# Layer 0's experts in two groups of batch elements

## The chip, the core and the metric

The kernel runs on one core of a Trainium2 chip. A core has a matrix engine (PE; its weight loads are shown apart as PEld), a vector engine (DVE), a scalar engine (ACT), a general one (POOL), and a queue engine (SP) that issues most transfers. Each engine works through its own instructions in order and waits for others on semaphores. Transfers run on 16 DMA engines that the queues share. The time is the device time of the whole program in microseconds (us), from the runs without a profile; the profile is one further execution, recorded instruction by instruction.

## What is computed

`x` has 16 batch elements of 128 tokens and 128 features. Four layers follow each other, each with an attention-like part and a feed-forward part, each added to `x` with a gate. The change touches layer 0. Its first part is a mixture of experts: a context picks two of eight experts for each token; its second part is a feed-forward whose hidden values are rounded to 8 bits.

```
logits = ctx @ Wg + bg                       # 8 experts
scores, idx = top_k(logits, 2); weights = softmax(scores)
h = relu(norm(x) @ W1[e] + b1[e])            # for the chosen experts e
x = x + tanh(g_xattn[0]) * sum(weights * (h @ W2[e] + b2[e]))

h = quantize(relu(norm(x) @ w1.T + b1))      # feed-forward of layer 0
x = x + tanh(g_ffn[0]) * quantize(h @ quantize(w2).T + quantize(b2))
```

Layer 1 follows with a block-sparse attention over `norm(x)` and the context.

## The kernel before

**Routing** (`l0_xattn`, lines 302 to 451). The normed rows of `x` are written to memory (`rows_d`). The two best experts of each token are found for all 16 batch elements at once. The 4096 pairs of token and expert are sorted by expert into blocks of 128 rows; each expert begins at a new block, so at most 2x16 + 7 = 39 blocks (`NBLK`) are needed. A running count over batch elements (`upto`, with `on` as its restart mask) gives each expert's number of blocks (`blocks`) and its last block (`ends`), `base` and `place` the row of each pair, `row` and `rows` the place from which its result is fetched later. `of` (the block of each pair, one-hot) and `os` (the row in it, one-hot) are multiplied on PE to turn this around: `tok` lists which row of `x` stands in which place of which block. The expert of each block is loaded into registers on SP, ACT and DVE (`numbers`).

**Blocks** (lines 453 to 504). `pipeline` runs four stages over the 39 blocks. At step t it calls `fetched(t)`, `turned(t-4)`, `hidden(t-5)` and `output(t-6)`. `fetched` gathers 128 rows by an indirect DMA from POOL (`l0_xs`, 4 buffers) and loads the expert's first weights, 258 KB, into one of `DEPTH = 7` places of `l0_w1` (tag `w16a`). `turned` transposes the rows and copies the second weights out of `w2` (tag `w16b`). `hidden` and `output` are two products of four 128x128 steps each, every one two passes on PE; `output` adds the bias and writes 64 KB to `out_d`. Every third block also lets one *position gather* go (`k.gather`): 65 gathers that fill `pe` for layer 2 and are spread over layers 0 and 1, each behind a given instruction.

**Returns** (`l0_returned`). For each batch element two indirect DMAs from POOL fetch the rows of both experts from `out_d`, and DVE adds each, weighted, to `x`. By `behind`, a gather waits for the add of the gather two before it. A return reads `out_d` as a whole and so waits for all blocks.

**Feed-forward** (`l0_ffn`). It goes by chunks of four batch elements. `hidden(j)` norms a chunk (with a square root on ACT), multiplies by `w1` (four 128x512 products of two passes), and rounds to 8 bits on ACT; `output(j)` multiplies by `w2` and adds to `x`. The returns of the next chunk are issued between the products. `turn_positions` transposes four matrices of `pe` and scales them, with PE and ACT; six such turns stand in chunks 1 to 3, eleven in layer 1's feed-forward.

**PSUM.** Eight banks are dealt out by tags, `mm=4, tr=2, acc=2`; a tag's banks go round. Before layer 1, `k.banks(bank=8)` closes this pool and opens one with a single tag.

**Order.** The program is written in the order of the calls; the build (`schedule_with_timeline_sim=True`) then places instructions in each engine's queue by a simulated time line, so that something written later can stand earlier if it is ready. The order is fixed when the kernel runs.

Of the kernel before, what the change touches and what calls it, by code (L numbers as in the profile page):

```python
# [63 lines left out]
class Kernel:  # L64


    def __init__(self, ctx, tc, a):
        self.tc, self.nc, self.a = tc, tc.nc, a
        pool = lambda name, bufs, **kw: ctx.enter_context(tc.tile_pool(name=name, bufs=bufs, **kw))
        self.const = pool("const", 1)  # L70
        self.wts = pool("weights", 1)
        self.work = pool("work", 2)
        self.small = pool("small", 3)
        self.psum_stack = ctx.enter_context(ExitStack())
        self.banks(mm=4, tr=2, acc=2)
# [206 lines left out]
def pipeline(n, *stages):  # L282
# [3 lines left out]
    for t in range(n + max(lag for _, lag in stages)):  # L286
        for s, (fn, lag) in enumerate(stages):
            u = t - lag
            if 0 <= u < n:
                kept[u, s] = fn(u, kept.pop((u, s - 1))) if s else fn(u)  # L290

def l0_xattn(k):

    nc = k.nc
    NBLK = 2 * NB + NE - 1  # L300
    M = 1.5 * 2.0**23
# [13 lines left out]
    nc.vector.memset(on, 1.0)  # L315
    nc.vector.memset(on[:, :, 0:1], 0.0)

# [43 lines left out]

    blocks, ends = k.sm([P, NE], "l0_blocks", bufs=1), k.sm([P, NE], "l0_ends", bufs=1)
    nc.vector.tensor_scalar(blocks, upto[:, :, NB - 1], 1.0 / P, 63.5 / P, ALU.mult, ALU.add)
# [36 lines left out]
    for n in range(2 * NB):  # L400
# [15 lines left out]
    ended = k.w2k("l0_ended")[:, : NBLK * NE].rearrange("p (n e) -> p n e", e=NE)  # L416
    nc.vector.tensor_tensor(
        ended, bc(k.iota[:, 0:NBLK].unsqueeze(2), [P, NBLK, NE]), bc(ends.unsqueeze(1), [P, NBLK, NE]), ALU.is_ge
    )
    whose = k.sm([P, NBLK], "l0_whose", bufs=1)  # L420
# [3 lines left out]
    k.l0_rows = rows = k.sm([P, 2 * NB], "l0_rows", I32, bufs=1)  # L424
    nc.vector.tensor_copy(rows, row)

# [16 lines left out]
    for n in range(0, NBLK, STEP):  # L443
        _, v = nc.values_load_multi_w_load_instructions(
            expert[0:1, n : n + STEP], [mybir.EngineType.SP, mybir.EngineType.Activation, mybir.EngineType.DVE],
            min_val=0, max_val=NE - 1,
            skip_runtime_bounds_check_because=known,
        )
        numbers += v
    out_d = k.dram.tile([NBLK * P, P], F32, name="l0_out_d")  # L450
    k.l0_out_d = out_d

# [37 lines left out]
    def output(n, args):  # L490
# [8 lines left out]
        )  # L499
        nc.sync.dma_start(out=out_d[n * P : (n + 1) * P], in_=y)  # L500
        if n % 3 == 2:
            k.gather(done)

    pipeline(NBLK, (fetched, 0), (turned, 4), (hidden, 5), (output, 6))


def l0_returned(k, b):
# [3 lines left out]
    for i in range(2):  # L511
        y = k.small.tile([P, P], F32, tag="l0_xs", name="l0_back", bufs=4)
        dma = nc.gpsimd.indirect_dma_start(  # L513
            out=y, out_offset=None, in_=k.l0_out_d,
            in_offset=bass.IndirectOffsetOnAxis(ap=k.l0_rows[:, 2 * b + i : 2 * b + i + 1].bitcast(U32), axis=0),
# [28 lines left out]

def l0_ffn(k):

# [42 lines left out]

    pipeline(NJ, (hidden, 0), (output, 1))  # L590

def l1_xattn(k):
# [8 lines left out]
    nc = k.nc  # L603
    k.banks(bank=8)
    H, DH, G = 16, 8, 4
# [187 lines left out]
def l1_ffn(k):  # L793
# [105 lines left out]
    for s in range(C * NJ + 24):  # L899
# [19 lines left out]
        for m, i in ms:  # L919
# [9 lines left out]
            elif i == C + 3:  # L929
                for fn, half in (  # L930
# [51 lines left out]
def l2_xattn(k):  # L982
# [239 lines left out]

    pipeline(NB // 2, (decays, 0), (scores, 1), (values, 2), (normed, 2), (added, 3))
    k.positions_stack.close()
# [3 lines left out]
def l2_ffn(k):  # L1228
# [85 lines left out]

    pipeline(NB, (one_hot, 0), (gather, 1))

# [24 lines left out]

    pipeline(2 * NE, (hidden, 0), (output, 1))

# [396 lines left out]

LAYERS = [l0_xattn, l0_ffn, l1_xattn, l1_ffn, l2_xattn, l2_ffn, l3_xattn]

# [85 lines left out]
```

## Time and profile before

| | us |
|---|---|
| runs without a profile: median of 3 (lowest, highest) | 897.01 (896.29, 897.06) |
| the profiled execution, whole | 889.87 |
| its span, first to last instruction | 888.2 |
| busy in the span: PE, PEld | 723.8, 483.2 |
| busy: DVE, ACT, POOL | 511.0, 402.5, 434.9 |
| mean granted clock of PE | 0.913 |
| first gather of a block, first product of a block | 47.1, 50.4 |
| last block written to `out_d`, first return issued | 132.0, 135.7 |
| last add of a return (start), last add of layer 0's feed-forward (start) | 191.7, 205.4 |
| first transpose of layer 1, first POOL operation of layer 1 | 203.7, 208.3 |

The three costliest POOL groups that matter here: 65 position gathers at 993 ns, 39 block gathers at 953 ns, 32 returns at 973 ns; that is the time POOL spends on issuing, not the transfer. A row of the time line has the start, the busy time, the engine, the line, the operation, the output and input names (numbers left out, so `l_xs` is `l0_xs`), and in brackets the idle time before it with what ended it. "Granted clock" is the share of full speed that PE was given. A stage's row in the table by windows has each engine's busy time and its count of instructions.

### The profile page before, as it was taken

The numbers are of one execution on the slowest core, as the hardware profiler recorded it, in microseconds if no ns is written. First come the engines' busy times: TensorE is split into PE (matmuls) and PEld (weight loads), VectorE is DVE, ScalarE is ACT, GpSimd is POOL, SyncE is SP. The second block draws the span as 40 slices with busy tenths as digits, with TensorE's granted clock in tenths as the row PEclk, the third lists the DMA queues.
The fourth block names the chain that finished last, engine by engine and source line by source line (L and its number), as shares of the span: only waits on it lengthen the run. The fifth ranks groups of instructions, "written<-read, shape, count | busy, mean of one in ns | idle before, by whom it ended". The sixth has DMA issues, their size and how long they took to land.

```text
span 888.2 us, 13281 instructions
## 1 busy us (share of the span) xinstructions
PE 723.8 (81%) x4349; PEld 483.2 (54%) x4349; DVE 511.0 (58%) x1450; ACT 402.5 (45%) x1006; POOL 434.9 (49%) x455
## 2 busy tenths in 40 slices
PE   3279990667897999899679799994789987999997
PEld 3179990343454555443268733333578885555555
DVE  5735543564645556788967235556541276777863
ACT  0035530332533545777316905631554455666552
POOL 6666655523754774777856603434120043555430
PEclk9989995876998999899959889996799999999999
DMA  8758861100000000000202203332000000000001
GB/s 256 208 131 212 206 157 39 41 22 16 16 16 20 22 25 22 0 0 1 71 25 85 73 3 97 94 83 94 0 1 1 1 1 1 1 1 0 1 1 48
DMA packets 43653, 46.49 MB, mean 52 GB/s; under 512 B 8368, under 2 KB 32560, under 8 KB 43456
## 3 DMA queue, kind: packets, MB, share of 16 engines
q1 hardware_dynamic: 37088, 35.63, 13.7%
q0 software_dynamic: 4384, 8.95, 4.4%
q10 hardware_dynamic: 2112, 1.05, 0.4%
q8 instruction: 35, 0.57, 0.3%
q14 instruction: 34, 0.28, 0.1%
HBM read 40.90 MB, written 4.72 MB: 51 GB/s over the span
## 4 chain that ended last, share of the span: by engine, by line
PE 50%; DVE 20%; POOL 7%; issue 7%; ACT 5%; DMA 4%; SPq 1%; POOLq 0%; DVEq 0%; ACTq 0%
PE ps_bank L38 17%; PE ps_bank L112 16%; PE ps_mm L112 10%; PE ps_acc L112 5%; POOL l_back L513 2%; DMA l_cm<-l_gm_d 2%; DMA l_back<-l_out_d,l_rows 2%; POOL l_ss L1212 2%; ACT l_cm L1155 2%; DVE l_m L38 2%; DVE l1f_r L38 1%; PE ps_bank L116 1%; DVE xnT L38 1%; PE ps_tr L116 1%; DVE l_up L38 1%
## 5 line engine op out<-in xcount | busy, mean ns | idle before, releaser
L962 POOL DMA_INDIRECT pe<-in_L_xattn_rpe,itokT x65 | 64.5, 993 | 63.1 <-DVE l_top L691 20.7
L38 PE MATMUL ps_bank<-xnT,l1f_w 128*128 128x512 f32 x128 | 62.5, 618 | 0.4 <-ACT pe L38 0.4
L691 DVE TENSOR_REDUCE l_top<-ps_bank 128x8 f32<-128x512 f32 x64 | 39.7, 683 | 34.1 <-PE ps_bank L112 34.1
L112 PE MATMUL ps_mm<-pe,ident 128*128 128x512 f32 x64 | 58.9, 1050 | 0.0
L723 ACT ACTIVATE l_a<-ps_bank 128x512 f32<-128x512 f32 x64 | 33.2, 602 | 45.8 <-PE ps_bank L112 45.7
L485 DVE TENSOR_SCALAR l_h<-ps_mm,l_w 128x128 f32<-128x128 f32 x117 | 33.7, 344 | 33.0 <-ACT l_h L487 32.1
L1148 POOL TENSOR_SCALAR_AFFINE_SELECT l_cm<-l_cm 128x512 f32<-128x512 f32 x32 | 23.7, 756 | 58.3 <-DMA l_cm<-l_gm_d 57.0
L1155 ACT ACTIVATE l_cm<-l_cm,l_g 128x128 f32<-128x128 f32 x128 | 39.8, 400 | 25.5 <-POOL l_cm L1148 25.5
L455 POOL DMA_INDIRECT l_xs<-l_rows_d,l_tok x39 | 37.2, 953 | 21.3 <-PE ps_acc L112 14.1
L112 PE MATMUL ps_acc<-l_w,l_h 128*128 128x128 f32 x312 | 45.6, 280 | 1.5 <-DVE l_y L497 1.3
L112 PE MATMUL ps_mm<-l_xT,l_w 128*128 128x128 f32 x312 | 44.4, 280 | 0.4 <-ACT l_xT L470 0.4
L112 PE MATMUL ps_mm<-l_qz,pe 128*128 128x128 f32 x256 | 38.3, 312 | 6.9 <-ACT pe L1102 6.9
L513 POOL DMA_INDIRECT l_back<-l_out_d,l_rows x32 | 31.1, 973 | 25.7 <-DVE x L520 19.0
L112 PEld LDWEIGHTS ps_acc<-l_w,l_h 128*128 128x128 f32 x312 | 40.0, 193 | 2.4 <-ACT l_h L487 2.3
L112 PEld LDWEIGHTS ps_mm<-l_xT,l_w 128*128 128x128 f32 x312 | 40.1, 197 | 0.6 <-ACT l_xT L470 0.6
L112 PEld LDWEIGHTS ps_mm<-l_qz,pe 128*128 128x128 f32 x256 | 36.0, 224 | 8.1 <-ACT pe L1102 8.1
L1328 ACT ACTIVATE l2f_h<-ps_bank,sb_L_ffn_b1T 128x264 f32<-128x264 f32 x64 | 28.1, 482 | 25.8 <-PE ps_bank L112 25.8
L1179 DVE TENSOR_TENSOR l_cm<-ps_mm,l_cm 128x512 f32<-128x512 f32 x32 | 22.0, 687 | 30.7 <-PE ps_mm L112 25.6
L38 PEld LDWEIGHTS ps_bank<-xnT,l1f_w 128*128 128x128 f32 x128 | 24.1, 200 | 24.9 <-issue 17.3
L38 POOL TENSOR_TENSOR l2f_o<-l2f_o,l2f_sc 128x264 f32<-128x264 f32 x9 | 6.5, 727 | 60.0 <-DVE l2f_o L38 57.2
L1337 DVE TENSOR_SCALAR l2f_y<-ps_bank,sb_L_ffn_b2T 128x264 f32<-128x264 f32 x16 | 7.9, 493 | 48.3 <-PE ps_bank L112 48.3
L38 PE MATMUL ps_bank<-xnT,sb_L_xattn_gru_whT 128*128 128x512 f32 x72 | 34.9, 593 | 0.0
(423 smaller groups left out, 1975.2 us busy)
## 6 DMA issues: line engine op xcount, KB each, us to landing
l_w<-in_L_xattn_w1b SPq DMA_DIRECT2D x39, 258.0 KB
l_cm<-l_gm_d SPq DMA_DIRECT2D x64, 128.0 KB
l_out_d<-l_y SPq DMA_DIRECT2D x39, 64.0 KB
sb_L_xattn_W<-in_L_xattn_W SPq DMA_DIRECT2D x1, 2048.0 KB
sb_L_ffn_w<-in_L_ffn_w SPq DMA_DIRECT2D x1, 2048.0 KB
pe<-in_L_xattn_rpe,itokT POOLq DMA_INDIRECT x65, 2.6
x<-in_x ACTq DMA_DIRECT2D x4, 256.0 KB
ctxT<-in_ctxT SPq DMA_DIRECT2D x1, 1024.0 KB
```

What stands on the lines that cost most here:

```text
L38: done = op(*args, **kw)
L112: self.nc.tensor.matmul(out, lhsT, rhs, start=start, stop=stop)
L455: nc.gpsimd.indirect_dma_start(out=xs, out_offset=None, in_=rows_d, in_offset=bass.IndirectOffsetOnAxis(ap=tok[:, n : n + 1].bitcast(U32), ...
L485: nc.vector.tensor_scalar(h[:, cols], ph[:, cols], bias, 0.0, ALU.add, ALU.max)
L513: dma = nc.gpsimd.indirect_dma_start(out=y, out_offset=None, in_=k.l0_out_d, in_offset=bass.IndirectOffsetOnAxis(ap=k.l0_rows[:, 2 * b + i ...
L691: done = nc.vector.tensor_reduce(top[:, 32 * g : 32 * g + 8], ss[g].rearrange("p (n s) -> p n s", n=8), AX.X, ALU.max)
L723: nc.scalar.activation(a, ss[g], AF.Exp, scale=scale)
L962: dma = nc.gpsimd.indirect_dma_start(out=k.pe[:, g if g < G - 1 else P - 1, :], out_offset=None, in_=k.a["L2_xattn_rpe"], in_offset=bass.I ...
L1148: nc.gpsimd.affine_select(out=by_n(cm), in_=by_n(cm), pattern=[[0, 4], [1, P]], compare_op=ALU.is_ge, fill=1e30, base=0, channel_multiplie ...
L1155: nc.scalar.activation(part, part, AF.Exp, scale=-1.0, bias=g[:, n : n + 1])
L1179: nc.vector.tensor_mul(cms[w], ps[w], cms[w])
L1328: nc.scalar.activation(h, ph, AF.Gelu, bias=b1[:, e * NF + f : e * NF + f + 1])
```

## The change

The batch elements are split: the first twelve (`SPLIT`) form group 0, the last four group 1. Each group is sorted into blocks of its own: 2x12 + 7 = 31 and 2x4 + 7 = 15, so `NBLK` is 46. `out_d` becomes two tensors. The restart mask, the block counts, the scans, `base`, `ended` and `rows` are worked out for each group. `of` grows from 39 to 46 columns and moves from a place of its own to the tag `w16a`, which `l0_w1` takes afterwards.

`pipeline` becomes a generator; `l0_xattn` yields for the first time after step 37, when block 31 has been put out, and then after each step. `l0_ffn` receives it and deals out in turn: for each of the first twelve batch elements two returns, one piece of each feed-forward chunk under way (`fed`), one step of the blocks; then the rest of the steps, then the returns of the last four elements, then the last chunk. A chunk is started when its four elements have returned. Its norm now takes the power -0.5 on POOL. Returns have buffers of their own (`l0_back`).

PSUM has one tag of eight banks from the start, and layer 1 opens no pool. Position gathers follow every second block of group 0 (15) in place of every third block (13). Seven position turns stand in layer 0 (one each in chunks 0 to 2, four in chunk 3), ten in layer 1's feed-forward.

```
-        self.banks(mm=4, tr=2, acc=2)
+        self.banks(bank=8)
...
-    NBLK = 2 * NB + NE - 1
+    SPLIT = NB - BJ
+    FIRST = 2 * SPLIT + NE - 1
+    NBLK = 2 * NB + 2 * (NE - 1)
+    groups = ((slice(0, SPLIT), slice(0, FIRST)), (slice(SPLIT, NB), slice(FIRST, NBLK)))
...
-    nc.vector.tensor_tensor_scan(ends, k.ones[:, 0:NE], blocks, 0.0, ALU.mult, ALU.add)
+    for g, (_, ns) in enumerate(groups):
+        nc.vector.tensor_tensor_scan(ends[:, g], k.ones[:, 0:NE], blocks[:, g], float(ns.start), ALU.mult, ALU.add)
...
-    nc.vector.tensor_tensor(base, base, bc(blocks.unsqueeze(2), [P, NE, NB]), ALU.add)
+    for g, (bs, _) in enumerate(groups):
+        part = base[:, :, bs]
+        nc.vector.tensor_tensor(part, part, bc(blocks[:, g].unsqueeze(2), list(part.shape)), ALU.add)
...
-    of = k.work.tile([P, 2 * NB, 2, NBLK], BF16, tag="l0_of", name="l0_of", bufs=1)
+    of = k.wts.tile([P, 2 * NB, 2, NBLK], BF16, tag="w16a", name="l0_of")
...
-        nc.sync.dma_start(out=out_d[n * P : (n + 1) * P], in_=y)
-        if n % 3 == 2:
+        g = int(n >= FIRST)
+        at = n - groups[g][1].start
+        nc.sync.dma_start(out=out_d[g][at * P : (at + 1) * P], in_=y)
+        if n % 2 and not g:
             k.gather(done)
-    pipeline(NBLK, (fetched, 0), (turned, 4), (hidden, 5), (output, 6))
+    for t in pipeline(NBLK, (fetched, 0), (turned, 4), (hidden, 5), (output, 6)):
+        if t >= FIRST + 6:
+            yield
...
-        y = k.small.tile([P, P], F32, tag="l0_xs", name="l0_back", bufs=4)
+        y = k.small.tile([P, P], F32, tag="l0_back", name="l0_back", bufs=4)
...
-    for b in range(BJ):
-        l0_returned(k, b)
     def hidden(j):
-        k.layernorm(j)
...
-            if j + 1 < NJ:
-                l0_returned(k, BJ * (j + 1) + f)
-            if j and f % 2:
-                turn_positions(k, 2 * (j - 1) + f // 2)
+            if j == NJ - 1 or f == 3:
+                turn_positions(k, j if j < NJ - 1 else NJ - 1 + f)
+            if f % 2:
+                yield
...
+    def fed(j):
+        yield from k.norm(j, pow=k.half)
+        yield
+        hq = yield from hidden(j)
+        yield
+        output(j, hq)
+
+    under_way = []
+    for b in range(NB - BJ):
+        l0_returned(k, b)
+        for f in under_way:
+            next(f, None)
+        next(blocks, None)
+        if b % BJ == BJ - 1:
+            under_way.append(fed(b // BJ))
+    for b in range(NB - BJ, NB):
+        next(blocks, None)
+        for f in under_way:
+            next(f, None)
+    for _ in blocks:
+        pass
+    for b in range(NB - BJ, NB):
+        for f in under_way:
+            next(f, None)
+        l0_returned(k, b)
+    for f in under_way + [fed(NJ - 1)]:
+        for _ in f:
+            pass
...
-    k.banks(bank=8)
...
-        if s % 2 and s // 2 <= P // 8 - 6:
-            turn_positions(k, s // 2 + 6)
+        if s % 2 and s // 2 <= P // 8 - 7:
+            turn_positions(k, s // 2 + 7)
...
+def l0(k):
+    blocks = l0_xattn(k)
+    next(blocks)
+    l0_ffn(k, blocks)
```

More of the change, by code (lines that the diff above doesn't have):

```diff
@@ L290, in pipeline @@
                 kept[u, s] = fn(u, kept.pop((u, s - 1))) if s else fn(u)
+        yield t
 def l0_xattn(k):
     nc = k.nc
-    NBLK = 2 * NB + NE - 1
+    SPLIT = NB - BJ
+    FIRST = 2 * SPLIT + NE - 1
+    NBLK = 2 * NB + 2 * (NE - 1)
+    groups = ((slice(0, SPLIT), slice(0, FIRST)), (slice(SPLIT, NB), slice(FIRST, NBLK)))
     M = 1.5 * 2.0**23
@@ L315, in l0_xattn @@
     nc.vector.memset(on, 1.0)
-    nc.vector.memset(on[:, :, 0:1], 0.0)
+    for bs, _ in groups:
+        nc.vector.memset(on[:, :, bs.start : bs.start + 1], 0.0)
     rows_d = k.dram.tile([NB * P, P], F32, name="l0_rows_d")
@@ L360, in l0_xattn @@
     nc.vector.tensor_sub(base, upto, base)
-    blocks, ends = k.sm([P, NE], "l0_blocks", bufs=1), k.sm([P, NE], "l0_ends", bufs=1)
-    nc.vector.tensor_scalar(blocks, upto[:, :, NB - 1], 1.0 / P, 63.5 / P, ALU.mult, ALU.add)
+    blocks, ends = k.sm([P, 2, NE], "l0_blocks", bufs=1), k.sm([P, 2, NE], "l0_ends", bufs=1)
+    for g, (bs, _) in enumerate(groups):
+        nc.vector.tensor_scalar(blocks[:, g], upto[:, :, bs.stop - 1], 1.0 / P, 63.5 / P, ALU.mult, ALU.add)
     nc.vector.tensor_scalar(blocks, blocks, M, None, ALU.add)
     nc.vector.tensor_scalar(blocks, blocks, -M, None, ALU.add)
-    nc.vector.tensor_tensor_scan(ends, k.ones[:, 0:NE], blocks, 0.0, ALU.mult, ALU.add)
+    for g, (_, ns) in enumerate(groups):
+        nc.vector.tensor_tensor_scan(ends[:, g], k.ones[:, 0:NE], blocks[:, g], float(ns.start), ALU.mult, ALU.add)
     nc.vector.tensor_sub(blocks, ends, blocks)
     nc.vector.tensor_scalar(blocks, blocks, float(P), -1.0, ALU.mult, ALU.add)
-    nc.vector.tensor_tensor(base, base, bc(blocks.unsqueeze(2), [P, NE, NB]), ALU.add)
+    for g, (bs, _) in enumerate(groups):
+        part = base[:, :, bs]
+        nc.vector.tensor_tensor(part, part, bc(blocks[:, g].unsqueeze(2), list(part.shape)), ALU.add)
     place = k.sq("l0_place")
@@ L416, in l0_xattn @@
     ended = k.w2k("l0_ended")[:, : NBLK * NE].rearrange("p (n e) -> p n e", e=NE)
-    nc.vector.tensor_tensor(
-        ended, bc(k.iota[:, 0:NBLK].unsqueeze(2), [P, NBLK, NE]), bc(ends.unsqueeze(1), [P, NBLK, NE]), ALU.is_ge
-    )
+    for g, (_, ns) in enumerate(groups):
+        part = ended[:, ns]
+        nc.vector.tensor_tensor(
+            part, bc(k.iota[:, ns].unsqueeze(2), list(part.shape)), bc(ends[:, g].unsqueeze(1), list(part.shape)),
+            ALU.is_ge,
+        )
     whose = k.sm([P, NBLK], "l0_whose", bufs=1)
@@ L424, in l0_xattn @@
     k.l0_rows = rows = k.sm([P, 2 * NB], "l0_rows", I32, bufs=1)
-    nc.vector.tensor_copy(rows, row)
+    for bs, ns in groups:
+        cols = slice(2 * bs.start, 2 * bs.stop)
+        nc.vector.tensor_scalar(rows[:, cols], row[:, cols], -float(P * ns.start), None, ALU.add)
     w = k.sm([P, NB, 2], "l0_w", bufs=1)
@@ L444, in l0_xattn @@
         _, v = nc.values_load_multi_w_load_instructions(
-            expert[0:1, n : n + STEP], [mybir.EngineType.SP, mybir.EngineType.Activation, mybir.EngineType.DVE],
+            expert[0:1, n : min(n + STEP, NBLK)], [mybir.EngineType.SP, mybir.EngineType.Activation, mybir.EngineType.DVE],
             min_val=0, max_val=NE - 1,
@@ L449, in l0_xattn @@
         numbers += v
-    out_d = k.dram.tile([NBLK * P, P], F32, name="l0_out_d")
-    k.l0_out_d = out_d
+    k.l0_out_d = out_d = [
+        k.dram.tile([(ns.stop - ns.start) * P, P], F32, name=f"l0_out{g}_d") for g, (_, ns) in enumerate(groups)
+    ]
     def fetched(n):
@@ L511, in l0_returned @@
     for i in range(2):
-        y = k.small.tile([P, P], F32, tag="l0_xs", name="l0_back", bufs=4)
+        y = k.small.tile([P, P], F32, tag="l0_back", name="l0_back", bufs=4)
         dma = nc.gpsimd.indirect_dma_start(
-            out=y, out_offset=None, in_=k.l0_out_d,
+            out=y, out_offset=None, in_=k.l0_out_d[int(b >= NB - BJ)],
             in_offset=bass.IndirectOffsetOnAxis(ap=k.l0_rows[:, 2 * b + i : 2 * b + i + 1].bitcast(U32), axis=0),
@@ L541, in l2_gates_of_ctx, with l0_ffn @@
     nc.vector.tensor_tensor(k.l2_gc, pg, bc(gb.unsqueeze(1), [P, NB, 2 * H]), ALU.add)
-def l0_ffn(k):
+def l0_ffn(k, blocks):
     nc = k.nc
@@ L588, in output @@
         k.add_chunk(j, y, 4)
-    pipeline(NJ, (hidden, 0), (output, 1))
+    def fed(j):
[25 more added lines that the diff above has]
+            pass
 def l1_xattn(k):
     nc = k.nc
-    k.banks(bank=8)
     H, DH, G = 16, 8, 4
@@ L1221, in added @@
         nc.vector.tensor_tensor(x, x, tb, ALU.add)
-    pipeline(NB // 2, (decays, 0), (scores, 1), (values, 2), (normed, 2), (added, 3))
+    for _ in pipeline(NB // 2, (decays, 0), (scores, 1), (values, 2), (normed, 2), (added, 3)):
+        pass
     k.positions_stack.close()
@@ L1313, in gather @@
         k.copy(tok[:, :, b, :], pg.rearrange("p (e c) -> p e c", e=NE))
-    pipeline(NB, (one_hot, 0), (gather, 1))
+    for _ in pipeline(NB, (one_hot, 0), (gather, 1)):
+        pass
     y = big.tile([P, NB, NE, CAP], F32, name="l2f_y")
@@ L1340, in output @@
         )
-    pipeline(2 * NE, (hidden, 0), (output, 1))
+    for _ in pipeline(2 * NE, (hidden, 0), (output, 1)):
+        pass
     AHEAD = NB * P // W
@@ L1738, in output @@
         k.add_chunk(j, y, 7)
-LAYERS = [l0_xattn, l0_ffn, l1_xattn, l1_ffn, l2_xattn, l2_ffn, l3_xattn]
+def l0(k):
+    blocks = l0_xattn(k)
+    next(blocks)
+    l0_ffn(k, blocks)
+LAYERS = [l0, l1_xattn, l1_ffn, l2_xattn, l2_ffn, l3_xattn]
 @with_exitstack
```

## The prediction

> **What bounds the kernel now.** I read the page's slices of the span first, then the busy time by stage, then the time line of layer 0, then the tiles of the two gathers. In slices of 22 us:
>
> ```profile
> PE   3279990667897999899679799994789987999997
> ...
> POOL 6666655523754774777856603434120043555430
> PEclk9989995876998999899959889996799999999999
> ```
>
> PE is full in slices 3 to 5 (the expert blocks), nearly empty in slice 6 and two thirds busy in 7 and 8, before layer 1 fills it. The stages one by one (columns: busy us of PE, PEld, DVE, ACT, POOL, then clock, DMA share, GB/s):
>
> ```profile
> 62.00:116.00 54.00, 52.50 (x466) 51.99 (x465) 28.65 (x108) 28.35 (x82) 34.66 (x37) 1.00 0.81 211
> ...
> 136.00:192.00 56.00, 25.25 (x100) 13.88 (x100) 26.93 (x101) 13.71 (x22) 30.85 (x32) 0.68 0.15 38
> 192.00:205.00 13.00, 9.03 (x40) 5.58 (x40) 8.09 (x33) 4.78 (x11) 0.00 (x0) 0.76 0.08 21
> ```
>
> The blocks are bound by PE: in the chain of waits three blocks take 5.69 us (98.73 to 104.42), so 1.90 each, at full clock. From 136 to 192 nothing is full. There the chain runs through the 32 returns:
>
> ```profile
> 135.72 3.80 DMA l_back<-l_out_d,l_rows x2
> 139.61 0.36 DVE x L520
> 140.70 0.95 POOL l_back L513
> 141.66 0.72 issue
> 142.60 0.95 POOL l_back L513
> ```
>
> A return waits for the add two returns earlier (`behind`, line 518). One lap, 139.36 to 142.60, is 3.24 us for two returns; the 16 laps from 135.72 to the last add at 192.09 average 3.5. How long a gather takes to land stands under each tile, first the blocks' `l_xs`, then `l_back`:
>
> ```profile
> DMA to landing us min/median/max: 3.1/3.9/5.0
> ```
>
> ```profile
> DMA to landing us min/median/max: 2.4/2.5/2.5
> ```
>
> A gather issued beside the blocks' weight loads lands 1.4 us later than one issued alone. That pair of rows decides most of the forecast. A lap is landing + 0.75: 0.1 to the add, 0.35 for it, 0.3 to the next issue (2.5 + 0.75 = 3.25, the lap seen).
>
> **The head.** It runs from the counts (27.5) to the token list (45.8), all in order on DVE. Added: one more `blocks` op, one more scan, and `base`, `ended` and `rows` split in two: five small ops at about 0.2 us start to start (27.54, 27.74, 27.94) = 1.0. `l_of` grows from 39 to 46 columns: (1.46 + 2x0.80 + 0.56) x 7/39 = 0.65. Seven more registers: the 1.17 us gap before line 390, x 7/39 = 0.2. Together +1.8 us, uncovered. The extra memset at the start is covered by DVE's 3.6 us wait for `x`.
>
> **The first weights.** `l_of` now takes the space of `l0_w1`. The queue issues the first loads at 34.20 today; they must then wait for the last matmul on `l_of` (44.5, or 46.3 with the head). Lost cover: 10 us of prefetch. Seven loads of 258 KB at 211 GB/s are 8.6 us; block 0 needs its load at 52.3, each later block 1.9 further, against 1.2 per load, so the loads themselves stay ahead. But the first `l_xs` then land beside them, 3.9 instead of 2.5: +1.4. Between 0 and +3 I take +1.
>
> **Pace of the first 31 blocks.** POOL issues a gather every 1.26 us (47.10, 48.36, 49.62). Today it makes 4 per 3 blocks, 5.0 of 5.69 us. With `n % 2` it makes 3 per 2 blocks, 3.78 against PE's 3.79: the slack is gone. A fetch that waits for its buffer (0.77 and 0.50 us per three blocks today) now shows. Between 0 and +2, I take +1; the two position gathers moved forward save nothing at the end, since they leave layer 1's feed-forward, whose critical engine is PE.
>
> **When the returns start.** Block 30's `y` is written at 116.1 today. From the last `y` (131.97) to the first return (135.72) are 3.75 us, write and landing. So 116.1 + 3.75 + 3.8 (head, weights, pace) = 123.6.
>
> **The window with both.** Until the second group's last output lie 15 blocks, feed-forward of chunks 0 and 1, two position turns and the gates of layer 2. PE: 15x1.90 = 28.5; a chunk at full clock is 8 matmuls at 0.43 + 0.9 + 0.5 = 4.8, twice 9.6; gates 3.9; turns 1: 43 us. POOL: 24 returns + 8 fetches at 1.26 + two `pow` at 1.05 = 42.4. DVE: 15x1.0 + 24x0.35 + two chunks at 5.3 (statistics 1.9, `xn` 1.1, copy 0.7, two ops of 0.7, the small ones) = 34. All three fit in 43 to 48 us only if none waits for another in order. The returns themselves: weight loads run only until block 45's is issued, seven blocks ahead of its use, so about three laps at 3.9 + 0.75 = 4.65 and nine at 3.4 + 0.3 for sharing DVE and POOL: 14 + 33.3 = 47.3, ending at 170.9. A fetch (1.26) and a `pow` fit into a lap's idle stretch on POOL, where today 0.7 to 1.1 us are idle after two issues. One `bank` tag of 8 binds the blocks to the feed-forward in program order, because a bank allotted to chunk 1's transpose holds up a block about 2.7 steps later until that chunk is normed (about 158): outputs end near 163, landed at 166, before 170.9.
>
> The Trainium skill ("DMA: Bandwidth & Descriptors", Anatomy of one DMA) puts such a gather at about 2.0 us plus its bytes at 436 GB/s, so 2.15 for 64 KB, and a lap at an estimated 2.9: twelve laps 35 us, 12 less than mine. The rows have 2.5 alone and 3.9 loaded, so they decide; the rule knows no neighbours. Against the change speaks "SBUF — State Buffer" (the box on DVE blocking DMA): while DVE runs a two-port fast mode, POOL can't write descriptors. The trace has such a case beside the bf16 work of line 395:
>
> ```profile
> 36.92 2.15 POOL L962 DMA_INDIRECT pe<-in_L_xattn_rpe,itokT  x1 [0.30 <-DVE l_o L403]
> ```
>
> 2.15 instead of 0.95. By the rule each norm's `xn` op could cost so much, 24 returns x 1.2 = 29 us at worst; but the return at 178.51 lies inside four such ops and took 0.95, and block ops read PSUM. I take 0.
>
> **Second group and tail.** Four laps of 3.3 = 13.2, and +1 for layer 1's memsets on POOL (line 637, 3.55 us, hidden at 124.9 today; `w2` is now free only among the returns; 0 to +3.5): last add at 185.1 against 192.1, **-7**. Behind it, chunk 3 pays `pow` (+0.5) and four turns instead of two (+1); but no pool of banks is closed before layer 1. Today `ps_bank` first appears at 203.67, when everything in layer 0 is done. Then a bank only waits for its own last user, so the projections (205.4 to 209.2) can slip under chunk 3's matmuls: -4 to -5. No row shows that; between +1.5 and -8 I take **-3**. The turn dropped from layer 1's feed-forward, 0.6 on PE, is left out.
>
> Sum: -7 - 3 = -10 on the profiled execution's 889.9 (span 888.2), so 879.9. The timed runs stand at 897.0, 7 above it; the same -10 gives **887**.
>
> **Rivals.** (a) *Laps stay long, slower.* The order on DVE is fixed at build. If adds stand ahead of block evictions, DVE parks until the gather lands, PE and the weight loads stretch with it, and landing stays at 3.9 with evictions queued before the adds. Break-even is 123.6 + 12 x lap + 14.2 = 195.1, a lap of 4.8. At 5.3: +6, 903. For it: 3.9 under load, DVE about 75% busy, order between four engines. Against: loads end early.
> (b) *Layer 1 starts much earlier.* Its first four batches need only chunk 0. If few banks are contended, they run under the last returns and laps are 3.4: 877. Against: chunk 3's ten bank allotments stand ahead of layer 1's in the rotation.
> (c) *It does not overlap.* If the order on POOL puts most returns behind the blocks, seven more blocks (13.3) and the head (1.8) stay, less 4 at the boundary: 908. Against: memset 637 was moved ahead of the returns, so order follows readiness.
> (d) *Even:* laps near 4.7, 897.
>
> **Chances.** Forecast 0.49, (a) 0.18, (b) 0.18, (c) 0.08, (d) 0.07. A measurement of this kernel can't tell less than about 0.2%, 1.8 us, from no change. Forecast and (b) are faster: 0.67; (d) 0.07; (a) and (c) 0.26. The range goes from 874 (laps of 3.4, the full -8 at the boundary) to 902 (laps of 4.8, memsets in the way, nothing gained at the boundary).
>
> **What the changed profile would show.** Step by step: first `l_back` issue near 124; landing of `l_back` with a median between 2.5 and 3.9; laps of 3.4 to 4.65; PE's clock at 1.0 up to 165; the last return's add near 185; first `l_qz` of layer 1 near 198 (208.25 today). The forecast is wrong if the laps exceed 4.8, if block 30 is written after 122, if second-group outputs come after 171, or if layer 1 loses what layer 0 gained.

## The result and the profile after

The changed kernel takes 903.5 us (median of four runs, 900.9 to 905.0) against 896.7 for the kernel before, run beside it: a ratio of 1.0103, 95% interval 1.0067 to 1.0138. It is 1% slower, where 887 and "faster" were forecast; the time lies just above the range.

The profiled execution took 900.92 us, span 899.2: 11.0 more than the one before. The medians lie only 6.9 apart, so about 4 us of the 11 are peculiar to the two profiled executions; the last section shows a piece of that size. PE's slices of 22 us:

```profile
PE   3269996836887999889668799994789987999997
```

Slices are counted from 0. Slice 6 of PE, nearly empty before, is now filled (0 became 6), so work does overlap there, and rival (c) is out; but slice 8, just ahead of layer 1, fell from 6 to 3. The same stages by windows (columns as before):

```profile
62.00:116.00 54.00, 51.76 (x444) 50.14 (x444) 27.81 (x104) 27.11 (x78) 36.72 (x40) 1.00 0.82 210
...
136.00:192.00 56.00, 39.00 (x253) 31.10 (x252) 33.38 (x131) 19.41 (x41) 36.27 (x39) 0.85 0.34 89
192.00:205.00 13.00, 5.80 (x14) 3.09 (x15) 4.58 (x23) 2.96 (x6) 2.09 (x3) 0.50 0.04 11
```

In the middle stage PE does 13.7 us more than before, but 17 of 56 us remain idle: nothing is full there, as before. In the last stage PE works at a granted clock of 0.50, where 0.76 was granted before. POOL's time line shows how the returns begin (start, busy time, engine, line, operation, names, and the idle time before with its releaser):

```profile
127.31 0.95 POOL L535 DMA_INDIRECT l_back<-l_out_d,l_rows  x1 [0.88 <-DVE x L542]
128.56 0.95 POOL L473 DMA_INDIRECT l_xs<-l_rows_d,l_tok  x1 [0.30 <-issue]
129.82 0.95 POOL L535 DMA_INDIRECT l_back<-l_out_d,l_rows  x1 [0.31 <-DVE l_h L503]
131.07 0.95 POOL L473 DMA_INDIRECT l_xs<-l_rows_d,l_tok  x1 [0.30 <-PE ps_bank L112]
132.33 0.95 POOL L535 DMA_INDIRECT l_back<-l_out_d,l_rows  x1 [0.30 <-issue]
133.58 0.95 POOL L473 DMA_INDIRECT l_xs<-l_rows_d,l_tok  x1 [0.30 <-PE ps_bank L112]
```

Each of these returns has a block's fetch behind it, so two returns take 5.0 us of POOL's issue alone; from 127.3 to 145.9 no gap between POOL's instructions is longer than 0.54 us. On DVE an add stands between the evictions of the blocks and holds them until its gather lands (three rows of DVE):

```profile
133.65 0.35 DVE L542 SCALAR_TENSOR_TENSOR x<-l_back,l_w,x 128x128 f32<-128x128 f32 x1 [2.55 <-DMA l_back<-l_out_d,l_rows]
...
134.32 0.85 DVE L503 TENSOR_SCALAR l_h<-ps_bank,l_w 128x128 f32<-128x128 f32 x3
...
139.49 0.35 DVE L542 SCALAR_TENSOR_TENSOR x<-l_back,l_w,x 128x128 f32<-128x128 f32 x1 [3.02 <-DMA l_back<-l_out_d,l_rows]
```

And PE, in the same stretch, first waits for such an eviction and then for a chunk's norm, while a block that is ready stands behind it in PE's order:

```profile
140.35 1.42 PE L112 MATMUL ps_bank<-l_w,l_h 128*128 128x128 f32 x6 [1.59 <-DVE l_h L503]
147.51 0.47 PE L116 MATMUL ps_bank<-ident,xn 128*128 128x128 f32 x1 [5.74 <-DVE xn L216]
147.78 0.42 PE L116 MATMUL ps_bank<-ident,l_xs 128*128 128x128 f32 x1
```

From the first group's last `y` (120.1) to the second group's (177.3) its 15 blocks so take 3.8 us each instead of 1.9. Later on POOL:

```profile
168.01 3.56 POOL L685 MEMSET l_v<- 128x2048 f32 x2
171.74 0.95 POOL L535 DMA_INDIRECT l_back<-l_out_d,l_rows  x1 [0.16 <-issue]
...
177.22 1.04 POOL L212 TENSOR_TENSOR ln_rs<-ln_rs,neg_half 128x4 f32<-128x4 f32 x1 [2.54 <-DVE ln_rs L211]
180.96 1.02 POOL L535 DMA_INDIRECT l_back<-l_out_d,l_rows  x1 [2.69 <-DMA l_out_d<-l_y]
```

Layer 1's memset stands between two returns, and the second group's first return waits for its rows. The milestones, from the time lines (us; starts, where no end is named):

| | before | after | forecast |
|---|---|---|---|
| last output of the first 31 blocks | 116.1 | 120.1 | 119.9 |
| first return | 135.7 | 124.2 | 123.6 |
| last add of the first group (end) | – | 176.3 | 170.9 |
| first return of the second group | – | 181.0 | about 171 |
| last add of all (end) | 192.1 | 195.3 | 185.1 |
| first `l_qz` of layer 1 | 208.3 | 215.2 | near 198 |
| DVE's first `xnT` copy in layer 1 | 216.4 | 226.8 | – |
| span | 888.2 | 899.2 | – |

Between these two executions eleven microseconds are lost: 3.2 up to the last add, 3.8 more up to layer 1's first `l_qz`, 3.3 more in layer 1's beginning, and 0.7 after that. The 3.3 are not the change's: the kernel before shows the same loss in its second trace (last section).

### The profile page after: what moved, and what is told of

The parts are those of the page before. It is cut to its first block, busy times and chain, and to the rows that moved or that the text cites. A ratio compares the mean times of both kernels' runs of the same rounds, so it can differ in the third digit from the quotient of the medians.

```text
span 899.2 us, 13623 instructions
## 1 busy us (share of the span) xinstructions
PE 734.6 (82%) x4468; PEld 496.2 (55%) x4468; DVE 520.7 (58%) x1480; ACT 408.4 (45%) x1023; POOL 442.2 (49%) x466
## 3 DMA queue, kind: packets, MB, share of 16 engines
q1 hardware_dynamic: 39104, 37.94, 14.4%
## 4 chain that ended last, share of the span: by engine, by line
PE 47%; DVE 22%; DMA 8%; issue 6%; ACT 6%; POOL 5%; SPq 0%; ACTq 0%; DVEq 0%; POOLq 0%
PE ps_bank L112 22%; PE ps_bank L38 15%; PE ps_mm L112 6%; DMA l_back<-l_out_d,l_rows 4%; ACT l_cm L1203 2%; PE ps_bank L116 2%; DMA l_cm<-l_gm_d 2%; DVE l_m L38 2%; DVE l1f_r L38 1%; DVE xn L216 1%; DVE xn L38 1%; PE ps_acc L112 1%; DMA l_out_d<-l_y 1%; POOL l_ss L1260 1%; DVE xnT L38 1%
## 5 line engine op out<-in xcount | busy, mean ns | idle before, releaser
L112 PE MATMUL ps_bank<-l_w,l_h 128*128 128x128 f32 x368 | 57.1, 285 | 5.3 <-DVE l_h L503 4.7
L503 DVE TENSOR_SCALAR l_h<-ps_bank,l_w 128x128 f32<-128x128 f32 x138 | 39.8, 343 | 35.3 <-ACT l_h L505 32.7
L38 PE MATMUL ps_bank<-xnT,l1f_w 128*128 128x512 f32 x128 | 59.7, 594 | 0.0
L112 PE MATMUL ps_bank<-l_xT,l_w 128*128 128x128 f32 x368 | 53.8, 292 | 1.7 <-ACT l_xT L488 1.5
L112 PEld LDWEIGHTS ps_bank<-l_w,l_h 128*128 128x128 f32 x368 | 50.7, 199 | 6.4 <-DVE l_h L503 5.7
L473 POOL DMA_INDIRECT l_xs<-l_rows_d,l_tok x46 | 43.8, 952 | 20.8 <-PE ps_bank L112 12.4
L112 PEld LDWEIGHTS ps_bank<-l_xT,l_w 128*128 128x128 f32 x368 | 48.7, 205 | 3.9 <-ACT l_xT L488 2.0
L505 ACT ACTIVATE l_h<-ps_bank,l_w 128x128 f32<-128x128 f32 x46 | 16.9, 368 | 46.1 <-PE ps_bank L112 35.9
L1260 POOL TENSOR_TENSOR l_ss<-l_ss,neg_half 128x16 f32<-128x16 f32 x8 | 23.3, 2915 | 26.8 <-DVE l_ss L1259 26.8
L116 PE MATMUL ps_bank<-ident,xn 128*128 128x128 f32 x36 | 10.5, 368 | 31.0 <-DVE xn L216 31.0
```

The source lines that it names most:

```text
L38: done = op(*args, **kw)
L112: self.nc.tensor.matmul(out, lhsT, rhs, start=start, stop=stop)
L116: self.nc.tensor.transpose(out, in_, self.ident[:n, :n])
L473: nc.gpsimd.indirect_dma_start(out=xs, out_offset=None, in_=rows_d, in_offset=bass.IndirectOffsetOnAxis(ap=tok[:, n : n + 1].bitcast(U32), ...
L503: nc.vector.tensor_scalar(h[:, cols], ph[:, cols], bias, 0.0, ALU.add, ALU.max)
L1260: nc.gpsimd.tensor_tensor(ss, ss, half, ALU.pow)
```

## The experiments

**How to compare them.** The runs fell on chips of two speeds: the kernel before took 894 to 897 us on some and 910 to 913 on others. On the slower ones the blocks' stage is longer: from 62 to 116 us the kernel before gets 406 matmuls done at 188 GB/s, against 466 at 211. So a ratio is always taken to the kernel before in the same company, and places in the trace are compared among chips of one speed. My two theories: *the laps bind* (loop of two returns, landing of the gathers, POOL's order), against *the second group's blocks bind* (PE and DVE late with them). Cost outside the overlap (seven more blocks, the one PSUM tag, the tail) was the third suspect.

All places, in us (starts); "–" where they were not read:

| kernel | before, same chip | ratio, 95% interval | first return | last `y` | last add | first `l_qz` |
|---|---|---|---|---|---|---|
| before | 896.7 | 1 | 135.7 | 131.7 | 191.7 | 208.3 |
| after | 896.7 | 1.0103 [1.0067, 1.0138] | 124.2 | 177.3 | 195.0 | 215.2 |
| e9_four_under_way | 893.7 | 1.0101 [1.0065, 1.0137] | 125.9 | 181.5 | 197.7 | 217.9 |
| e10_old_banks | 893.7 | 1.0049 [1.0022, 1.0075] | – | – | – | – |
| e11_banks_first_turns_four | 893.7 | 0.9975 [0.9958, 0.9992] | 125.6 | 161.3 | 184.7 | 205.5 |
| e12_before_four | 893.7 | 0.9861 [0.9825, 0.9898] | 136.2 | 131.6 | 178.7 | 195.1 |
| b2_before | slower chips from here | – | 146.4 | 141.7 | 202.6 | 219.4 |
| a2_after | 910.8 | 1.0082 [1.0062, 1.0102] | 131.8 | 190.6 | 207.8 | 227.5 |
| e1_turns | 912.8 | 1.0055 [1.0028, 1.0083] | 132.5 | 192.9 | 209.5 | 228.0 |
| e2_blocks_first | 912.8 | 1.0063 [1.0041, 1.0085] | 133.8 | 174.1 | 208.3 | 229.1 |
| e5_two_steps | 910.8 | 1.0069 [1.0050, 1.0088] | 131.2 | 175.5 | 206.2 | 227.6 |
| e8_first_turns | 910.8 | 1.0043 [1.0020, 1.0066] | 132.0 | 172.9 | 208.4 | 227.5 |
| e3_before46 | 912.8 | 1.0116 [1.0081, 1.0151] | 164.1 | 160.1 | 220.2 | 236.6 |
| e4_before_banks | 912.8 | 1.0102 [1.0081, 1.0124] | 154.9 | 150.9 | 209.5 | 232.2 |
| e13_sqrt | 910.2 | 1.0080 [1.0054, 1.0106] | 132.5 | 194.1 | 211.3 | 229.6 |
| e14_first_four | 910.2 | 0.9993 [0.9975, 1.0011] | 131.4 | 181.1 | 198.6 | 220.9 |
| e15_all_sqrt | 910.2 | 1.0025 [1.0009, 1.0041] | 134.7 | 178.6 | 203.7 | 223.9 |
| e17_before_pow | 910.2 | 1.0038 [1.0021, 1.0054] | 147.4 | 142.8 | 202.9 | 220.6 |
| e18_four_edits_power | 909.7 | 1.0048 [1.0028, 1.0068] | 134.0 | 177.9 | 202.4 | 226.2 |
| e19_four_edits_root | 909.7 | 1.0013 [0.9997, 1.0028] | 134.2 | 177.3 | 203.0 | 222.7 |

### What parts of the change cost by themselves

**Seven more blocks.** The kernel before with 46 blocks in one group, the seven added ones without rows of their own, and `of` in the weights' place (a loop's end is also cut to `NBLK`):

```
-    NBLK = 2 * NB + NE - 1
+    NBLK = 2 * NB + 2 * (NE - 1)
...
-    of = k.work.tile(..., tag="l0_of", name="l0_of", bufs=1)
+    of = k.wts.tile(..., tag="w16a", name="l0_of")
```

> The kernel before with 46 blocks in place of 39 (seven more, empty ones) and the one-hot table in the space of the first weights; one group, nothing overlapped. Prices the added work alone: seven blocks at 1.90 us are 13.3, the later weight loads 2.4 and the wider head about 0, so 15 to 16 us over before. If the added work were free beside the returns, nothing would show here either; if the blocks are bound by PE, the first return moves from 135.7 to about 151.

1.0116, or 10.6 us, less than the 15 to 16 expected. In the traces the last add comes 17.6 us later than in the kernel before (b2), layer 1's last `l_qT` copy 13.4 and the end 11.0. Of what seems made good there, 3.4 us is the group of the last section, long in b2's trace and short in this one. This cost is what the overlap had to earn before it gained anything.

**One PSUM tag of eight.** The kernel before with `banks(bank=8)` from the start and no pool closed ahead of layer 1:

```
-        self.banks(mm=4, tr=2, acc=2)
+        self.banks(bank=8)
...
-    k.banks(bank=8)
```

> The kernel before with one tag of eight banks from the start and no pool closed ahead of layer 1. The prediction took 4 to 5 us from this boundary (projections of layer 1 under chunk 3): the first masked query of layer 1 would move from 208.3 to about 204. Theory D (the order on DVE puts the norm for layer 1 behind the last feed-forward op anyway): it stays at 208.3 within 1 us and the time within 1.5 us of before.

1.0102: it costs as much as the whole change, where I had booked a gain of 4 to 5 us and theory D expected no change. A row of PE's waits says how (who waited for whom, us in total, times, longest):

```profile
PE ps_bank L112 <- ACT l_xT L470: 11.3, 7, 1.7
```

In the blocks' stage (62 to 140) PE waits 11.3 us, seven times, for a copy of `l_xT`; with 46 blocks and the three tags (e3), on the same chip, no such row stands there, and PE gets 387 matmuls done from 62 to 116 against 371 here.

At the end, PE's time line:

```profile
222.00 1.95 PE L112 MATMUL ps_bank<-l_wq,l0f_q 128*128 128x128 fp8e4 x32
227.39 0.99 PE L116 MATMUL ps_bank<-ident,xn 128*128 128x128 f32 x3 [3.44 <-DVE xn L216]
```

Both last chunks' second products (32 = 2x16) stand in one piece behind the last chunk's first products, so that layer 1's first transpose waits for two chunks: from the last add to the first `l_qz` it is 22.7 us instead of 16.8 (b2). With tags of their own the stages had been kept apart.

**The power.** The kernel before with POOL's power in place of ACT's square root in layer 0's feed-forward norms:

```
     def hidden(j):
-        k.layernorm(j)
+        k.layernorm(j, pow=k.half)
```

> The kernel before, with only the power in place of the square root in layer 0's feed-forward norms. GpSimd has about 1 us idle per lap there, so the first three powers are hidden; the last chunk's takes 1.04 in place of 0.3, and the table load, at 151 us today where nothing waits for it, falls into the tail. If that is a cost of its own: first l_qz 2 to 4 us later than before, ratio 1.002 to 1.005. If it costs only in company with the split: ratio 0.999 to 1.001.

1.0038, within what the first theory said, though the traces show only 1.2 us at the first `l_qz`, less than its 2 to 4. ACT's load of the function table for the square root (1.28 us), at 161.75 in b2's trace, now stands at 204.13, right behind the last add.

### What holds the last add

**The blocks' steps listed ahead of the returns**, in the kernel after; and **two steps of the blocks for each batch element**:

```
+    for _ in blocks:
+        pass
     under_way = []
     for b in range(NB - BJ):
```

> All remaining block steps are written ahead of the returns and the feed-forward. Theory A (the second group is late because feed-forward and returns stand ahead of ready blocks in the queues of PE and DVE): the last y of the second group moves from 177 to about 155 to 162, the first return of the second group from 181 to the end of the first group's returns, about 172 to 176, and the time falls by 5 to 9 us. Theory B (engines are simply full, so order doesn't matter): the last y stays within 3 us of 177 and the time within 2 us.

```
         next(blocks, None)
+        next(blocks, None)
         if b % BJ == BJ - 1:
```

> The changed kernel with two block steps dealt out per batch element instead of one, so blocks stand further ahead in the queues but feed-forward still stands between them. Theory A: between the change and blocks first, last y of the second group 8 to 12 us earlier than in the change, ratio about 1.007. Theory B (engines full): ratio 1.010.

The changed kernel and the kernel before were run once more beside the second of them:

> The changed kernel, unchanged, beside the others on one chip. The ratio to before was 1.0103; theory A and C together expect 1.010 again here, and the last y of the second group some 20 us after the same block would come at the blocks' own pace.

> The kernel before, unchanged, to have a trace from the same chip as the other runs. If the blocks' stage took longer in the last runs because this chip moves data more slowly, the first return comes at about 143 here instead of 135.7; if the edits did it, at 135.7.

The two edits bring the last `y` forward by 15 to 17 us (190.6 to 174.1 and 175.5). The last add stays within 2 us (207.8; 208.3 and 206.2), and the time falls by only 1 to 2 us against a2, where 5 to 9 were expected of the first edit. So the second group's lateness, which looks like the cause in the changed kernel's POOL rows, is not the only limit: when the blocks are early, the returns still in their loop take until then.

**Four returns under way**, in the kernel after:

```
-        if len(k.l0_added) > 1:
-            k.behind(dma, k.l0_added[-2])
+        if len(k.l0_added) > 3:
+            k.behind(dma, k.l0_added[-4])
```

> The kernel after, with a return waiting for the add four returns earlier in place of two. If the time between two returns is landing plus the add in a closed loop of two (my forecast's lap), this halves what a lap costs: the 24 returns of group 0 take about 45 us in place of 70, last add 6 us or more earlier, ratio 1.000 or less. If the returns are held by what stands between them on GpSimd and VectorE (fetches that wait for a buffer, adds behind block operations), they shorten by less than 5 us, and the ratio stays at 1.006 to 1.010.

1.0101, as the change itself (1.0103): nothing gained, against the lap theory. The trace (POOL's time line) shows why:

```profile
166.86 0.94 POOL L535 DMA_INDIRECT l_back<-l_out_d,l_rows  x1 [0.30 <-issue]
167.85 3.55 POOL L685 MEMSET l_v<- 128x2048 f32 x2
...
185.96 1.02 POOL L535 DMA_INDIRECT l_back<-l_out_d,l_rows  x1 [11.39 <-DMA l_out_d<-l_y]
```

The first group's last return now goes at 166.9 instead of 173.2, and then POOL waits 11.4 us for the second group, whose blocks have become 4.2 us later (181.5). Each limit covers the other.

**Both at once**, nothing else:

> The kernel after with two edits only: the blocks' steps listed ahead of the returns, and four returns under way. Each alone left the last add where it was (195 to 198 us on a chip of this speed, or 208 on the slower one): with the blocks first the returns ended last, with four under way the blocks did. If the two limits cover each other, both edits give a last add below 188 although the one tag of eight banks stays, and a ratio to before of 0.998 to 1.003. If the one tag is the third limit, the last add stays above 192 and the ratio at 1.005 or more.

0.9993 against 1.0082: the two edits, worth about 0.2% (not clear of noise) and nothing alone, pay 0.9% together. The last add is 9.2 us earlier than in the changed kernel on a chip of this speed (198.6 against 207.8; the 188 and 192 of the expectation were meant for the faster chips). So about half of what the forecast missed (0.989 forecast, 1.0082 here) is the interlock of loop and order, and it goes without touching the one tag. One gap stays: four under way was run alone on a fast chip only, the blocks first and the pair on slower ones, and what an edit is worth can differ between them.

**The same loop in the kernel before**, the edit of e9 alone:

> The kernel before, with a return waiting for the add four returns earlier. With POOL's 0.95 us of issue and 0.31 between issues as the only limit, 32 returns take 40 us in place of 56; layer 0's feed-forward chunks then end last in their own order, 4.8 us each at full clock. If the closed loop of two is the bound of that stage: ratio 0.985 to 0.993. If the adds and the norm chain on VectorE bound it: above 0.996.

0.9861: 12.4 us faster than before, near the better end of what the first theory said, and the fastest kernel of all. Its POOL:

```profile
136.23 0.95 POOL L513 DMA_INDIRECT l_back<-l_out_d,l_rows  x1 [3.10 <-issue]
137.49 0.95 POOL L513 DMA_INDIRECT l_back<-l_out_d,l_rows  x1 [0.30 <-issue]
138.75 0.95 POOL L513 DMA_INDIRECT l_back<-l_out_d,l_rows  x1 [0.30 <-issue]
140.01 0.95 POOL L513 DMA_INDIRECT l_back<-l_out_d,l_rows  x1 [0.30 <-DMA l_back<-l_out_d,l_rows]
```

A return every 1.26 us, where two took 3.25 to 3.5 before: 32 of them in 40 us, and the last add at 178.7 instead of 191.7. The distance from there to layer 1 is the old one (16.4 against 16.5). About 13 of the 56 us that the change wanted to hide were a wait that the program itself had asked for; the rest is now POOL's issue.

### The turns, the tags and the root in the kernel after

**Turns out of chunk 3**: two in each of chunks 0 to 2, and the seventh back in layer 1's feed-forward; then the same with the blocks first:

```
-            if j == NJ - 1 or f == 3:
-                turn_positions(k, j if j < NJ - 1 else NJ - 1 + f)
+            if j < NJ - 1 and f % 2:
+                turn_positions(k, 2 * j + f // 2)
...
-        if s % 2 and s // 2 <= P // 8 - 7:
-            turn_positions(k, s // 2 + 7)
+        if s % 2 and s // 2 <= P // 8 - 6:
+            turn_positions(k, s // 2 + 6)
```

> The changed kernel with six position turns in chunks 0 to 2 and none in chunk 3 (eleven again in layer 1's feed-forward). Theory T (the four turns lie on the path of the last chunk): in the changed kernel the span from the copy of the last normed chunk to the last rounding took 8.1 us against 4.1 before, so this falls to about 4.5 and the time by 3 us, to about 900 where the changed kernel has 903.5. Rival (ACT's and PE's turns hide in the cold matmuls): no change in that span, time within 1 us.

> Both edits together: block steps written ahead of returns and feed-forward, and no turns in chunk 3. The two gave 1.0063 and 1.0055 alone where the change had 1.0103. If they act on separate stretches (blocks' end, tail), they add up: 1.0015, so about the time of before. If the second only fills what the first leaves idle: 1.005.

1.0055 against 1.0082 for the change, and 1.0043 with the blocks first. The intervals of e1 and a2 overlap, so a gain of 0.3% isn't clear of noise, and the trace speaks against theory T: without the turns the last chunk's eight first products take 6.8 us, where a2 has 7.1 with turns between them and the kernel before 4.1. PE is granted a clock of 0.53 there (208 to 222), in a2 0.66. The turns stand in a stretch that is slow without them too.

**Three tags again** in the kernel after:

```
-        self.banks(bank=8)
+        self.banks(mm=4, tr=2, acc=2)
...
+    k.banks(bank=8)
     H, DH, G = 16, 8, 4
```

> The kernel after, with the three PSUM tags of before (mm 4, tr 2, acc 2) and the pool closed ahead of layer 1. If the one tag of eight banks is what costs (in the kernel before it cost 1.0% alone): blocks back at 2.35 us each on this chip instead of 2.5, last y about 8 us earlier, first return 4 to 5 us earlier, ratio to before 0.997 to 1.003. If the lock-step of returns and blocks is what costs and the tag only matters where the blocks alone run: first return earlier, last add within 2 us of the changed kernel's (207.8 on this chip), ratio 1.006 to 1.010.

1.0049, against 1.0101 for e9 on the same chip and 1.0103 for the change: about half a per cent, half of what the tag cost in the kernel before, and between the ranges of the two theories.

**Four edits at once**: three tags, blocks first, turns out of chunk 3, four under way.

> The kernel after with all four edits: three PSUM tags, the blocks' steps listed ahead of the returns, the position turns taken from chunk 3, four returns under way. If the losses add up (tag 1.0%, turns and order 0.4%, loop 0 to 0.6%): ratio 0.990 to 0.997, faster than both kernels. If they are covers of one another, ratio 1.000 to 1.004.

0.9975 on a fast chip: 0.25% ahead of the kernel before, and 1.2% behind e12. Its last add ends at 185.1, the very place forecast for the change; but the first `l_qz` follows at 205.5, not at 198. DVE's rows show where that tail is held:

```profile
185.74 0.23 DVE L259 TENSOR_SCALAR ln_rs<-ln_mv 128x4 f32<-128x4 f32 x2
187.80 0.27 DVE L261 RECIPROCAL ln_rs<-ln_rs 128x4 f32<-128x4 f32 x2 [1.83 <-ACT ln_rs L260]
190.01 0.69 DVE L605 TENSOR_TENSOR l0f_y<-ps_acc,l_bq 128x512 f16<-128x512 f32 x1 [1.93 <-PE ps_acc L112]
190.62 1.11 DVE L216 TENSOR_SCALAR xn<-x,ln_mv,ln_rs 128x128 f32<-128x128 f32 x4
```

The last chunk's `xn`, whose power POOL finished at 187.0, stands behind the square roots of *layer 1's* norms (L260 and L261, which need ACT's table load, 1.28 us at 186.27) and behind chunk 2's output: 5.5 us from the last add to `xn`, against 1.3 before. Hence the next edit.

**The square root again**, alone in the kernel after and beside the four edits:

```
-        yield from k.norm(j, pow=k.half)
+        yield from k.norm(j)
```

> The kernel after, with only the norms of layer 0's feed-forward by square root. No power on GpSimd among the returns (three of 1.0 us), no table load in the tail. If these matter by what they last: 3 us earlier at the last add, 1.3 less between it and xn, ratio 1.003 to 1.006. If the returns are held by other things: last add within 1 us, ratio 1.007 to 1.009.

> Three PSUM tags, blocks first, turns out of chunk 3, four under way, and layer 0's feed-forward norms by ScalarE's square root again in place of GpSimd's power. With the power, the four edits gave 0.9975, the last add 7 us before that of before and the first l_qz only 2.8 before. If the power's moved table load (1.28 us on ScalarE, beside the last add) is what keeps the rest: last chunk's xn within 2 us of the last add in place of 5.5, first l_qz at 198 to 202, ratio 0.988 to 0.994. If the tail is long for another reason: first l_qz 20 us behind the last add again, ratio 0.996 to 0.999.

Alone it gives nothing (1.0080 against 1.0082), though the tail is 1.4 us shorter than in a2 (18.3 against 19.7): the last add had come 3.5 later. With the four edits it gave 1.0025, on a slower chip than e11, so the two can't be compared. Both were then run on one chip:

> The four edits (three PSUM tags, blocks first, turns out of chunk 3, four under way) with the power, once more, this time on the same chip as the square root in its place. If the difference of 0.9975 and 1.0025 was the chips' (before 894 on one, 910 on the other): this one lands at the other's ratio on a slow chip, 1.000 to 1.004, or again at 0.996 to 0.999 on a fast one, and the two differ by less than 0.2%. If the power is the better half of the split: it is ahead by 0.3 to 0.5% here too.

> The four edits with the square root, on the same chip as with the power. If the moved table load is a cost by itself here, as it was in the kernel before (1.0038): 0.3 to 0.4% faster than with the power. If what the list of instructions puts in which order outweighs it: slower than with the power by up to 0.5%.

1.0048 and 1.0013 on that chip: the root is 0.35% ahead, about the price of the power in the kernel before (0.38%). Their two traces also differ in the 3.4 us of the last section; how much of the medians' difference that is, no run shows. And the four edits that were ahead of the kernel before on a fast chip (0.9975) are behind it on a slow one (1.0048). On slow chips e14 with one tag (0.9993) even stands better than e18 with three tags and the turns moved (1.0048): these edits don't add up. That each changes the order that the build lays down may be why; it isn't shown.

## Why the prediction was wrong

The step that failed is "The window with both". It said that all three engines "fit in 43 to 48 us only if none waits for another in order", and then reckoned with one such wait only, a bank held until chunk 1 is normed, and with outputs near 163. The engines wait for each other far more: from the first return to the second group's last output it took 53.4 us (124.2 to 177.6), of which PE was busy for 42.9. The second term to fail is the boundary to layer 1, put at -3 and measured at +3.8.

On the profiled execution I forecast 879.9 and 900.9 came: 21.0 off (16.5 on the medians, 903.5 against 887). Up to the end of the last add it is 10.2 (195.3 against 185.1), from there to layer 1's first `l_qz` 6.8, and after it 4.0, of which 3.4 is the group of the last section.

- **The head, the first weights and the pace** were forecast at +1.8, +1 and +1. The first `l_xs` went 0.6 earlier instead (46.51 against 47.10). The split operations did cost 0.6 and the wider `l_of` 1.0, but the whole chain began 0.7 earlier (25.81 against 26.54), and the 1.17 us gap ahead of `l_of`, which I had let grow, was gone (31.82 to 33.16 before, 31.67 to 31.87 after); why, no run shows. The first weights cost about 3: the first transpose starts at 51.98 (49.60 before), after a gather that took 5.4 us beside the late loads. The pace took 1.7. That the first return, forecast at 123.6, went at 124.2 is luck: the errors cancel.
- **"A fetch (1.26) and a `pow` fit into a lap's idle stretch on POOL"** failed first. I counted eight fetches against 24 returns and did not ask where they would stand: one behind each of returns 3 to 8, so two to a lap, 4x1.26 = 5.0 us. Landing did what I had put: in the chain of waits two early returns take 3.74 and 4.55 us to their adds beside the last weight loads, the rest mostly 2.5 to 3. The twelve laps and the memset between them took 52.0 us, not 47.3.
- **"Outputs end near 163, landed at 166, before 170.9."** They ended at 177.6, and the second group's first return waited until 181.0, 10 us later than forecast. The busy time that I added up for PE was right (43 us); that the engines would overlap freely was not. DVE parks at an add (2.55 and 3.02 us in the rows above), PE at an eviction (1.59) and at a norm (5.74), POOL at PE. Outputs after 171 were one of my own signs of being wrong. e2, e9 and e14 show that neither side alone was the limit.
- **The second group's four laps** were right: 14.4 us against 13.2 + 1, but the memset that the 1 stood for lay in the first group.
- **"-4 to -5" for the pool of banks that is no longer closed** had no row behind it, as I said there, and the sign was wrong. Layer 1's first `xn` stands on DVE behind chunk 3's output both before (202.58, then 203.19) and after (209.87, then 210.48), so nothing slips under. e4 priced the whole tag at +1.0%, with 5.9 us between the last add and `l_qz`; e10 at half that.
- **`pow` at +0.5 and four turns at +1** were too small: 1.3 from the last add to `xn` (2.6 against 1.3; the table load of the square root now stands there, at 196.23), and 2.4 behind it. PE's time line of the tail after:

```profile
198.41 1.16 PE L116 MATMUL ps_bank<-ident,xn 128*128 128x128 f32 x4 [12.56 <-DVE xn L216]
200.35 2.07 PE L112 MATMUL ps_bank<-xnT,sb_L_ffn_w1T 128*128 128x512 f32 x2 [0.78 <-DVE xnT L109]
202.22 1.06 PE L116 MATMUL ps_bank<-ident,pe 128*128 128x128 f32 x4
203.07 1.91 PE L112 MATMUL ps_bank<-xnT,sb_L_ffn_w1T 128*128 128x512 f32 x2
```

  The turns (`pe`) now stand between the last chunk's products; the two of before ran while `xnT` was copied. After 12.6 idle us PE runs the first products at half clock (0.50 granted from 200 to 205), 2.07 for two that take 1.02 from 207.13 on. By e1 the half clock weighs more than the turns: taking them out left the eight products at 6.8 us.
- **Rival (a)** named the mechanism, adds ahead of evictions with DVE parked, and its 903 is the time that came, by luck: its arithmetic wasn't the reason. The laps averaged 4.3 with the memset, below its break-even of 4.8. What decided was what it left out as well, the second group's lateness and the tail.
- **The two-port rule** against the change was weighed at 0, and that was right: the 32 returns took 939 to 1037 ns to issue. My one case for it (36.92, 2.15 us) proves little: the operations of line 395 beside it are `tensor_tensor`, and no run shows whether they use the fast mode that the rule speaks of.

The loop of two (line 518) stood in my working as the very lap I was counting. I never asked what undoing it would bring; e12 answers 12.4 us.

## What to carry to other kernels

When a stage is bound by nothing, look first for a wait that the program itself asked for (here a hand-written dependence two steps back), and price its removal before any rearrangement. When two stages are laid over each other on engines that work in order, the sum of busy times is only the floor: write down who stands behind whom on each engine, and expect two limits that hide each other, so that mending either alone can show next to nothing. Sharing one rotation of buffers among stages, or moving a norm to another engine, is no neutral clean-up: here the one cost 1.0% by itself and the other 0.4%.

## What was not expected of the hardware

The largest piece of layer 1's loss is one group of four operations, and it comes and goes by itself. DVE's row after, then the same group in b2, the kernel before on another chip, then POOL's rows after:

```profile
221.66 4.56 DVE L216 TENSOR_SCALAR xn<-x,ln_mv,ln_rs 128x128 f32<-128x128 f32 x4
```

```profile
225.26 4.47 DVE L216 TENSOR_SCALAR xn<-x,ln_mv,ln_rs 128x128 f32<-128x128 f32 x4
```

```profile
223.09 1.05 POOL L752 TENSOR_TENSOR l_mz<-l_topT,l_neg 128x512 f32<-128x512 f32 x1
224.09 1.04 POOL L712 TENSOR_TENSOR l_qz<-l_qT,mask8x 128x512 f32<-128x512 f32 x1
225.08 1.04 POOL L712 TENSOR_TENSOR l_kz<-l_kT,mask8x 128x512 f32<-128x512 f32 x1
```

Four `xn` operations took 4.56 us, one of them 3.76, where the same four took 1.13 in the first trace of the kernel before (214.74). In all twenty traces the same POOL operations stand beside this group; it takes 4.5 to 4.6 us in nine of them (the two above, a2, e1, e2, e5, e9, e10, e18) and 1.1 in eleven. So it is no effect of the change, and two single traces can differ by 3.4 us, 0.4%, through it alone. The long one ends 0.1 us behind the last of three products that POOL ran back to back. The Trainium skill ("SBUF — State Buffer", Who interferes with whom) says that when a DVE operation in a two-port mode and one of POOL's meet, whichever issues first gets the shared ports for its whole instruction and the other is blocked. The end fits that, but the wait outlasts three POOL instructions of 1.04 us, and no run varied their order or shows the mode, so the cause is argued, not shown.

The gathers' landing row for the returns is 2.5/2.5/2.8 in the changed kernel, yet the chain counts 3.74 and 4.55 for two of them: that row doesn't cover every gather, and the adds' own waits are the better measure.

Chips differ by 1.8% for one and the same kernel (894 and 910 us), and the worth of an edit can differ with them: the four edits stand at 0.9975 on one and at 1.0048 on another.
